# Loading the first batch alone, and projecting it in parts between the first attention items

## The chip, the cores and the metric

The kernel runs on one core of a Trainium2 chip. The metric is the device time of one execution in microseconds (us); before the change it is 2163.86 us, the median of three runs (2162.97 to 2166.31). The core has engines that run their own instruction queues side by side: TensorE for matrix products (PE in the profile, PEld for its weight loads), VectorE (DVE), ScalarE (ACT), GpSimd (POOL) and SyncE (SP), which here only issues transfers. ScalarE can issue transfers too. The queues meet through semaphores, on which an instruction waits for another engine or for a transfer to land.

## The reference, cut to what matters

The input `x` has 4 batches of 128 channels and 64 x 64 places, so N = 4096 tokens of 128 channels. Everything is in 32-bit floats.

```python
# layer 0: attention over all tokens, 64 inner channels
q, k, v = wq @ xf, wk @ xf, wv @ xf           # per batch: 64 x 4096
att = softmax(k.T @ q, axis=2)                # 4096 x 4096
x = x + wo @ (att @ v.T).T
# layer 1: tokens, layer norm, causal attention with 128 channels
t = tokens(x)
h = layer_norm(t)
t = t + softmax(causal((h @ Wq) @ (h @ Wk).T * 128**-0.5)) @ (h @ Wv)
# then a recurrence over the tokens
wx = batch_norm(layer_norm(t) @ W.T)          # statistics over all batches and tokens
y[i] = sigmoid(wx[i] + y[i-1] @ V.T)
out = from_tokens(t + y)
```

## The kernel before

The work is done in `fast_path`. A second path, `general_path`, runs only if a flag computed at the end says that the first one left its numeric range.

**Storage.** `xs` holds all four batches of `x` in on-chip memory, first as channels by tokens. Once the projections of a batch have read a block of 512 tokens, `tokens0` (L510) overwrites that block with the same data as tokens by channels, from a second input `xT`; the residual is added to it there. `kr` holds, for each half of the sequence, keys in one half of the partitions and rows (the queries' side) in the other; `swap` is a copy of `kr` with the two halves of the partitions exchanged, made by a transfer (L482), so that products over 64 channels can run on both halves of the array at once. `v` holds the values by tokens.

**Projections of a batch.** `keys(b, m)` (L750) returns three tasks for part `m` of four. Part `m` covers block `m` of 512 tokens and block `m + 4`. `cols0` multiplies both blocks by `wqk` and `wkq`, copies the results into `kr` by VectorE and ScalarE and starts the two `swap` transfers. `vals0` computes values, `vals0_by_tokens` transposes them. All of these take their PSUM tiles from `misc`, a ring of two buffers.

**Items.** The attention of both layers is cut into items: one block of 512 rows (`g`) against two tiles of 128 keys. Layer 0 of a batch has 8 blocks of 16 items; item `k` uses key tiles `k` and `k + 16`, so items 0 to 3 of a block need part 0 of the projections, items 4 to 7 part 1, and so on. Layer 1 follows for the same batch, and then the next batch. The loop at L774 goes over slots. In each, `scores` of item `s` (products and the exponential), `values` of item `s - 2`, and `sums` of item `s` are written out. At a block's last item, `rows()` (L764) prepares the block after the next, and for layer 0 also starts its token load; `finish0` or `finish1` are put into `waiting` to run a few slots later. A slot with nothing due takes one task from the list `side`. In the kernel before, the projections of batches 1 to 3 go through `side` during block 1 of the previous batch's layer 1 (L779 to L781), and those of batch 0 are all written ahead of the loop (L758 to L760).

**The opening.** Weights are loaded by ScalarE's queue (L398), `x` in sixteen loads of 512 KB by SyncE's queue (L407 to L409), all batches at once. The first product on TensorE is layer 1's combined weight `g1` = `wqT` times `wkT` (L453 to L455), read first by `rows1` in layer 1. The order of instructions on each engine is chosen by a scheduler that goes by the order of the program and by what is ready.

Of the kernel before, what the change touches and what calls it, by code (L numbers as in the profile page):

```python
# [9 lines left out]
F32 = mybir.dt.float32  # L10
# [5 lines left out]
P = 128  # L16
BLK = 512
CHUNK = 1024
# [331 lines left out]
def fast_path(  # L350
# [21 lines left out]
    nc = tc.nc  # L372
    B, C, N = x.shape
    M = c_wqT.shape[1]
    assert C == P and M == P // 2 and N % CHUNK == 0
    NT = N // P
    NB = N // BLK
# [7 lines left out]
    const = ctx.enter_context(tc.tile_pool(name="const", bufs=1))  # L385
# [5 lines left out]
    xs = xpool.tile([P, B, N], F32, name="xs")  # L391

    x2 = dram.tile([B, N, P], F32, name="x2")

    def load(name, shape, *parts):
        t = const.tile(shape, F32, name=name)
        for dst, src in parts:
            nc.scalar.dma_start(out=dst(t), in_=src)  # L398
        return t

    whole = lambda t: t
    lo, hi = (lambda t: t[:, 0:M]), (lambda t: t[:, M:P])
    top, bottom = (lambda t: t[0:M]), (lambda t: t[M:P])
    wqk = load("wqk", [P, P], (lo, c_wqT), (hi, c_wkT))
    wkq = load("wkq", [P, P], (lo, c_wkT), (hi, c_wqT))
    wv0 = load("wv0", [P, M], (whole, c_wvT))
    for b in range(B):  # L407
        for g in range(N // CHUNK):
            nc.sync.dma_start(out=xs[:, b, ts(g, CHUNK)], in_=x[b, :, ts(g, CHUNK)])  # L409
    wo2 = load("wo2", [P, P], (top, c_woT), (bottom, c_woT))  # L410
    wqT = load("wqT", [P, P], (whole, a_wqT))
    wkT = load("wkT", [P, P], (whole, a_wkT))
    wv1 = load("wv1", [P, P], (whole, a_wv))
    wf = load("wf", [P, P], (whole, f_wT))
    vf = load("vf", [P, P], (whole, f_vT))
    gamma = load("gamma", [P, 1], (whole, f_gamma))
    beta = load("beta", [P, 1], (whole, f_beta))

    ident = const.tile([P, P], F32, name="ident")
    make_identity(nc, ident)  # L420
# [5 lines left out]
    nc.gpsimd.memset(mhalf, -0.5)  # L426
    minus = const.tile([P, P], F32, name="minus")
    nc.vector.tensor_scalar(minus, ident, -1.0, None, ALU.mult)
    good = const.tile([P, 1], F32, name="good")
    g1 = const.tile([P, P], F32, name="g1")  # L430
    recs = const.tile([P, 2, B, NT], F32, name="recs")
# [10 lines left out]
    with tc.tile_pool(name="batch", bufs=1) as batch, tc.tile_pool(name="rows", bufs=2) as rowp, tc.tile_pool(  # L442
        name="prob", bufs=4
    ) as prob, tc.tile_pool(name="work", bufs=2) as wk, tc.tile_pool(name="stat", bufs=4) as stat, tc.tile_pool(
        name="ps_s", bufs=2, space=PSUM
    ) as ps_s, tc.tile_pool(name="ps_a", bufs=1, space=PSUM) as ps_a, tc.tile_pool(
        name="ps_m", bufs=2, space=PSUM
    ) as ps_m:

        def misc(name):  # L450
            return ps_m.tile([P, BLK], F32, tag="m", name=name)

        gp = misc("g_ps")  # L453
        nc.tensor.matmul(gp[:, :P], lhsT=wqT, rhs=wkT, start=True, stop=True)
        nc.vector.tensor_copy(g1, gp[:, :P])  # L455

        class Batch:
            pass
# [1 line left out]
        bs = [Batch() for _ in range(B)]  # L460
# [4 lines left out]
        def cols0(b, m):  # L465

            bt = bs[b]
            if m == 0:  # L470
                bt.kr = batch.tile([P, 2, N // 2], F32, tag="kr", name="kr")
                bt.swap = batch.tile([P, N // 2], F32, tag="swap", name="swap")
                bt.v = batch.tile([P, NT, M], F32, tag="v", name="v0")
            for h, w in enumerate((wqk, wkq)):
                ps = misc("kr_ps")
                nc.tensor.matmul(ps, lhsT=w, rhs=xs[:, b, ts(m + h * NB // 2, BLK)], start=True, stop=True)
                if h:
                    nc.scalar.copy(bt.kr[:, h, ts(m, BLK)], ps)
                else:
                    nc.vector.tensor_copy(bt.kr[:, h, ts(m, BLK)], ps)  # L480
                rows, keys = slice(M - h * M, P - h * M), slice(h * M, h * M + M)
                nc.sync.dma_start(out=bt.swap[keys, ts(m, BLK)], in_=bt.kr[rows, h, ts(m, BLK)])  # L482

        def vals0(b, m):

            ps = misc("v_ps")
            for h in range(2):
                nc.tensor.matmul(
                    ps[h * M : h * M + M], lhsT=wv0, rhs=xs[:, b, ts(m + h * NB // 2, BLK)], start=True, stop=True
                )  # L490
            vT = wk.tile([P, BLK], F32, tag="vT", name="vT")
            nc.scalar.copy(vT, ps)
            return vT

        def vals0_by_tokens(b, m, vT):
            ps = misc("vT_ps")
            for j in range(TPB):
                nc.tensor.transpose(ps[:, ts(j, P)], vT[:, ts(j, P)], ident)
            v = bs[b].v.rearrange("p (h t) c -> p t h c", h=2)[:, ts(m, TPB)]
            nc.scalar.copy(v, ps.rearrange("p (t h c) -> p t h c", h=2, c=M))  # L500
# [9 lines left out]
        def tokens0(b, g):  # L510

            nc.sync.dma_start(
                out=xs[:, b, ts(g, BLK)].rearrange("p (j c) -> p j c", c=P),
                in_=xT[b, ts(g, BLK)].rearrange("(j p) c -> p j c", p=P),
            )
# [111 lines left out]
        items, blocks = [], []  # L627
# [58 lines left out]
        def sums(it):  # L686

            if it.first:
                bs[it.b].dsum = wk.tile([P, 2, BLK], F32, tag="dsum", name="dsum")
            it.den = den = bs[it.b].dsum  # L690
            if all(n == BLK for _, _, n, _ in it.at):
                flat = den.rearrange("p a b -> p (a b)")
                if it.first:
                    nc.vector.tensor_copy(flat, it.p)  # L694
                else:
                    nc.vector.tensor_tensor(flat, flat, it.p, ALU.add)  # L696
                return
            for h, (t, q0, n, o) in enumerate(it.at):
                if it.first:
                    if q0:  # L700
                        nc.gpsimd.memset(den[:, h, :q0], 0.0)
                    nc.vector.tensor_copy(den[:, h, q0:], it.p[:, o : o + n])
                else:
                    nc.vector.tensor_tensor(den[:, h, q0:], den[:, h, q0:], it.p[:, o : o + n], ALU.add)  # L704
# [40 lines left out]
        def push(slot, chain):  # L745
            step = next(chain, None)
            if step:
                waiting.append((slot + step[0], step[1], chain))

        def keys(b, m):  # L750
            mem = []
            return [
                lambda: cols0(b, m),
                lambda: mem.append(vals0(b, m)),
                lambda: vals0_by_tokens(b, m, mem[0]),
            ]

        for m in range(NB // 2):  # L758
            for task in keys(0, m):
                task()  # L760
        SKEW = 2
        side = []

        def rows():  # L764

            if blocks:
                layer, b, g = blocks.pop(0)
                (rows1 if layer else rows0)(b, g)
                if layer == 0:
                    tokens0(b, g)  # L770

        rows()
        rows()
        for s in range(len(items) + SKEW + 16):  # L774
            if s < len(items):
                it = items[s]
                if it.first:
                    bs[it.b].rows = bs[it.b].next.pop(0)
                    if it.layer and it.g == 1 and it.b + 1 < B:  # L779
                        for m in range(NB // 2):  # L780
                            side += keys(it.b + 1, m)  # L781
                scores(it)
            if 0 <= s - SKEW < len(items):
                it = items[s - SKEW]
                values(it)
                if it.last:
                    rows()
                    if fill:
                        fill.pop(0)()
                    push(s, (finish1 if it.layer else finish0)(it.b, it.g))  # L790
            if s < len(items):
                sums(items[s])
            due = [w for w in waiting if w[0] <= s]
            if due:
                w = min(due, key=lambda w: w[0])
                waiting.remove(w)
                w[1]()
                push(s, w[2])
            elif side:
                side.pop(0)()  # L800
        assert not waiting and not side and not fill


# [4 lines left out]
    with tc.tile_pool(name="xr", bufs=1) as xrp, tc.tile_pool(name="y", bufs=2) as yp, tc.tile_pool(  # L808
        name="ps_y", bufs=1, space=PSUM
# [21 lines left out]
        start = xrp.tile([P, B, NCH + 1], F32, name="start")  # L831
# [130 lines left out]
```

## Time and profile before

| | |
|---|---|
| time, median of three | 2163.86 us |
| profiled span | 2161.9 us |
| `x` loads: number, size, median issue to landing | 16, 512 KB, 7.7 us |
| token loads `xT`: number, size, median | 32, 256 KB, 3.3 us |
| `swap` transfers: number, size, median | 32, 128 KB, 2.2 us |
| exponential of layer 0, 128x1024 (L670): mean | 1116 ns |
| running sums, 128x1024 (L696): mean | 1225 ns |
| score and value records of layer 0, 64x512 (L656, L716): mean | 593 and 591 ns |

A line of the timeline gives the start in us, the busy time in us, the engine, the line of the kernel, the operation, what it writes and reads, its shape, and how many instructions are merged in it; in brackets stands how long the engine was idle before it and who released it. "SPq" and "ACTq" are transfers being issued by SyncE and ScalarE. One 32-bit product appears as two PE records. Records overlap: a 512-column record lasts 592 ns, but the next begins 0.43 us after it. The table of stretches gives the stretch, its length, then for each engine the busy time and the count, then the granted clock, the busy share of the transfer engines and what they moved. The 128 KB of `swap` counts one transfer of L482.

### The profile page before, as it was taken

To read this page: it belongs to the slowest core of one execution; us is meant where nothing else is said; L and a number is where in the kernel's file an instruction comes from. 1 tells how busy PE (TensorE), PEld (TensorE's weight loads), DVE (VectorE), ACT (ScalarE), POOL (GpSimd) and SP (SyncE) were. 2 spreads that over 40 slices of the span, in tenths; PEclk is the share of its full clock that TensorE was granted. 3 is DMA by queue.
4 is the path that set the end of the run, shared out by engine and by line. 5 is a ranking of instruction groups with operands and counts; after the bars stand their busy time and mean duration, and the time that the engine had idled before them with its cause. 6 is when DMAs were issued, how large, how long until landed. Compare 5 with 4: busy or idle time off the path is not lost. (4 is left out here: it accounts for less than half of the span.)

```text
span 2161.9 us, 30424 instructions
## 1 busy us (share of the span) xinstructions
PE 2115.7 (98%) x12204; PEld 941.5 (44%) x12204; DVE 1435.2 (66%) x2703; ACT 1007.9 (47%) x1098; POOL 104.5 (5%) x207
## 2 busy tenths in 40 slices
PE   7999999999999999999999999999999999999978
PEld 2333354444333344444333335444433334544446
DVE  3888865444788876554588886544478887654468
ACT  4666633323566643333466663323356664333255
POOL 0000010000000010000000001000000001000000
PEclk9999999999999999999999999999999999999989
DMA  6000011000000001100000001100000000000033
GB/s 224 2 1 2 1 30 49 5 6 5 6 2 1 1 20 30 34 5 5 6 1 2 1 1 30 49 5 5 5 6 2 1 2 6 10 10 5 5 161 157
DMA packets 42997, 48.72 MB, mean 23 GB/s; under 512 B 3168, under 2 KB 36704, under 8 KB 40800
## 3 DMA queue, kind: packets, MB, share of 16 engines
q1 hardware_dynamic: 40960, 46.15, 6.4%
q8 instruction: 97, 1.59, 0.3%
q10 hardware_dynamic: 1888, 0.56, 0.1%
q14 instruction: 52, 0.43, 0.1%
HBM read 25.72 MB, written 16.78 MB: 20 GB/s over the span
## 5 line engine op out<-in xcount | busy, mean ns | idle before, releaser
L696 DVE TENSOR_TENSOR dsum<-dsum,p 128x1024 f32<-128x1024 f32 x676 | 827.9, 1225 | 464.3 <-ACT p L672 335.4
L670 ACT ACTIVATE p<-s_ps,nshift 128x1024 f32<-128x1024 f32 x512 | 571.2, 1116 | 357.7 <-PE s_ps L656 338.2
L672 ACT ACTIVATE p<-s_ps 128x1024 f32<-128x1024 f32 (+2 forms) x288 | 274.2, 952 | 598.8 <-PE s_ps L665 496.1
L716 PE MATMUL acc<-p,v 64*64 64x512 f32 x4096 | 533.2, 591 | 1.7 <-ACT half L735 1.7
L656 PE MATMUL s_ps<-swap,kr 64*64 64x512 f32 x2048 | 528.5, 593 | 0.4 <-ACT p L670 0.4
L656 PE MATMUL s_ps<-kr 64*64 64x512 f32 x2048 | 528.5, 593 | 0.0
L665 PE MATMUL s_ps<-rows,xhT 128*128 128x512 f32 (+3 forms) x1152 | 503.9, 559 | 0.0
L724 PE MATMUL acc<-p,xh 128*128 128x512 f32 (+3 forms) x1152 | 501.5, 557 | 0.0
L724 PEld LDWEIGHTS acc<-p,xh 128*128 128x128 f32 x1152 | 215.6, 190 | 241.3 <-issue 231.8
L665 PEld LDWEIGHTS s_ps<-rows,xhT 128*128 128x128 f32 x1152 | 211.0, 190 | 227.1 <-issue 189.7
L716 PEld LDWEIGHTS acc<-p,v 64*64 64x64 f32 x4096 | 155.2, 133 | 284.8 <-issue 265.8
L656 PEld LDWEIGHTS s_ps<-swap,kr 64*64 64x64 f32 x2048 | 137.0, 133 | 131.3 <-issue 124.2
L656 PEld LDWEIGHTS s_ps<-kr 64*64 64x64 f32 x2048 | 137.0, 133 | 128.3 <-issue 123.7
L436 POOL TENSOR_TENSOR ln_rstd<-ln_var,mhalf 128x4 f32<-128x4 f32 x64 | 66.1, 1033 | 1217.8 <-DVE ln_var L551 1217.8
L704 DVE TENSOR_TENSOR dsum<-dsum,p 128x256 f32<-128x256 f32 (+1 forms) x120 | 56.0, 499 | 72.0 <-POOL p L676 72.0
L694 DVE COPY dsum<-p 128x1024 f32<-128x1024 f32 x60 | 41.4, 690 | 66.8 <-ACT p L672 57.1
L539 DVE SCALAR_TENSOR_TENSOR xs<-o_ps,recs,xs 128x128 f32<-128x128 f32 x256 | 73.0, 345 | 8.9 <-PE o_ps L534 2.8
L555 DVE TENSOR_SCALAR xh<-xs,ln_mv,ln_rstd 128x128 f32<-128x128 f32 x256 | 71.4, 343 | 2.2
L676 POOL TENSOR_SCALAR_AFFINE_SELECT p<-p 128x128 f32<-128x128 f32 x128 | 34.4, 293 | 672.7 <-ACT p L672 672.7
L548 DVE BATCH_NORM_STATS2 ln_st<-xs 128x6 f32<-128x128 f32 x256 | 63.6, 271 | 0.0
L861 DVE SCALAR_TENSOR_TENSOR z<-xs,scale,y_ps 128x256 f32<-128x256 f32 x108 | 48.6, 481 | 6.7 <-PE y_ps L859 5.4
L614 ACT COPY xs<-wx_ps 128x512 f32<-128x512 f32 x32 | 18.7, 585 | 73.1 <-DVE stats L612 73.1
(104 smaller groups left out, 1058.7 us busy)
## 6 DMA issues: line engine op xcount, KB each, us to landing
xs<-in_x SPq DMA_DIRECT2D x16, 512.0 KB, 7.7
xs<-in_xT SPq DMA_DIRECT2D x32, 256.0 KB, 3.3
x<-xs SPq DMA_DIRECT2D x32, 256.0 KB, 2.3
xr<-x SPq DMA_DIRECT2D x8, 1024.0 KB, 11.9
out_x<-xr SPq DMA_DIRECT2D x8, 1024.0 KB, 4.4
swap<-kr SPq DMA_DIRECT2D x32, 128.0 KB, 2.2
wo<-in_c_woT ACTq DMA_DIRECT2D x2, 32.0 KB, 4.3
wqT<-in_a_wqT ACTq DMA_DIRECT2D x1, 64.0 KB, 5.2
```

What stands on the lines that cost most here:

```text
L436: nc.gpsimd.tensor_tensor(y, var, mhalf[:, : y.shape[-1]], ALU.pow)
L539: nc.vector.scalar_tensor_tensor(t, in0=op[:, ts(j, P)], scalar=rec[:, j : j + 1], in1=t, op0=ALU.mult, op1=ALU.add)
L548: nc.vector.bn_stats(st[:, j], xs[:, b, ds(g * BLK + j * P, P)])
L555: nc.vector.tensor_scalar(dst[:, j], xs[:, b, ds(g * BLK + j * P, P)], mv[:, j, 0:1], y[:, j : j + 1], ALU.subtract, ALU.mult)
L656: nc.tensor.matmul(ps[c * M : c * M + M, off : off + n], lhsT=bs[it.b].kr[part, h, ds(t % (NT // 2) * P + c * M, M)], rhs=rows[h], start=True,
L665: nc.tensor.matmul(ps[:, off : off + n], lhsT=lhsT, rhs=rhs, start=True, stop=True)
L670: nc.scalar.activation(it.p[:, :off], ps[:, :off], AF.Exp, bias=nshift)
L672: nc.scalar.activation(it.p[:, :off], ps[:, :off], AF.Exp, scale=float(P) ** -0.5)
L696: nc.vector.tensor_tensor(flat, flat, it.p, ALU.add)
L704: nc.vector.tensor_tensor(den[:, h, q0:], den[:, h, q0:], it.p[:, o : o + n], ALU.add)
L716: nc.tensor.matmul(bt.acc[h * M : h * M + M, r], lhsT=bt.v[part, t], rhs=it.p[part, o : o + n], start=it.first, stop=it.last,)
L724: nc.tensor.matmul(bt.acc[:, 0, q0:], lhsT=bt.xh[:, t], rhs=it.p[:, o : o + n], start=it.first and h == 0, stop=it.last and h == 1,)
```

## The change

At the start only batch 0 is loaded, in eight loads of 512 tokens, ordered by the parts of the projection that need them. The loads of `wo2`, `wqT`, `wkT` and `wv1` move from ScalarE's to SyncE's queue, behind `x`; `wf`, `vf`, `gamma` and `beta` are loaded later, by `load_rest`. The next batch's `x` is loaded while layer 0 of the current batch is at work: a small GpSimd copy out of `agg` into the region that the load will overwrite makes the load wait until that block's result exists. Twelve products of the identity with itself, whose result nothing reads, occupy TensorE until `x` comes. Of batch 0's projections only part 0 and the keys of part 1 are written ahead of the loop; the rest goes into `side`, one task a slot in the first block, and last `form`, which computes `g1`. The token loads of the first two blocks of batch 0 are put off until these tasks are done. The purpose is to let the items start sooner.

```diff
-    def load(name, shape, *parts):
+    def load(engine, name, shape, *parts):
...
-    for b in range(B):
-        for g in range(N // CHUNK):
-            nc.sync.dma_start(out=xs[:, b, ts(g, CHUNK)], in_=x[b, :, ts(g, CHUNK)])
...
+    for m in range(NB // 2):
+        for g in (m, m + NB // 2):
+            nc.sync.dma_start(out=xs[:, 0, ts(g, BLK)], in_=x[0, :, ts(g, BLK)])
+    wo2 = load(nc.sync, "wo2", [P, P], (top, c_woT), (bottom, c_woT))
+    wqT = load(nc.sync, "wqT", [P, P], (whole, a_wqT))
+    wkT = load(nc.sync, "wkT", [P, P], (whole, a_wkT))
+    wv1 = load(nc.sync, "wv1", [P, P], (whole, a_wv))
...
-        gp = misc("g_ps")
-        nc.tensor.matmul(gp[:, :P], lhsT=wqT, rhs=wkT, start=True, stop=True)
-        nc.vector.tensor_copy(g1, gp[:, :P])
+        wp = misc("warm_ps")
+        for _ in range(12):
+            nc.tensor.matmul(wp[:, :P], lhsT=ident, rhs=ident, start=True, stop=True)
+
+        def form():
+            gp = misc("g_ps")
+            nc.tensor.matmul(gp[:, :P], lhsT=wqT, rhs=wkT, start=True, stop=True)
+            nc.vector.tensor_copy(g1, gp[:, :P])
+
+        def load_rest():
+            for t, src in ((wf, f_wT), (vf, f_vT), (gamma, f_gamma), (beta, f_beta)):
+                nc.sync.dma_start(out=t, in_=src)
...
-        for m in range(NB // 2):
-            for task in keys(0, m):
-                task()
+        parts = [keys(0, m) for m in range(NB // 2)]
+        for task in parts[0][:2] + parts[1][:1] + parts[0][2:]:
+            task()
         SKEW = 2
-        side = []
+        side = parts[1][1:] + parts[2] + parts[3] + [form]
...
                 if layer == 0:
-                    tokens0(b, g)
-
+                    started.append((b, g))
+
+        def tokens():
+
+            while started:
+                b, g = started.pop(0)
+                tokens0(b, g)
+                if g == 2 and b + 1 < B:
+
+                    nc.gpsimd.tensor_copy(
+                        xs[:, b + 1].rearrange("p (k n) -> p k n", n=CHUNK)[:, :, 0], bs[b].agg[:, : N // CHUNK]
+                    )
+                    for k in range(N // CHUNK):
+                        nc.sync.dma_start(out=xs[:, b + 1, ts(k, CHUNK)], in_=x[b + 1, :, ts(k, CHUNK)])
...
                 if it.last:
                     rows()
+                    tokens()
...
             elif side:
                 side.pop(0)()
+                if not side and items[s].b == 0 and items[s].layer == 0:
+                    tokens()
+                    load_rest()
```

More of the change, by code (lines that the diff above doesn't have):

```diff
@@ L393, in fast_path @@
     x2 = dram.tile([B, N, P], F32, name="x2")
-    def load(name, shape, *parts):
+    def load(engine, name, shape, *parts):
         t = const.tile(shape, F32, name=name)
         for dst, src in parts:
-            nc.scalar.dma_start(out=dst(t), in_=src)
+            engine.dma_start(out=dst(t), in_=src)
         return t
@@ L403, in fast_path @@
     top, bottom = (lambda t: t[0:M]), (lambda t: t[M:P])
-    wqk = load("wqk", [P, P], (lo, c_wqT), (hi, c_wkT))
-    wkq = load("wkq", [P, P], (lo, c_wkT), (hi, c_wqT))
-    wv0 = load("wv0", [P, M], (whole, c_wvT))
-    for b in range(B):
-        for g in range(N // CHUNK):
-            nc.sync.dma_start(out=xs[:, b, ts(g, CHUNK)], in_=x[b, :, ts(g, CHUNK)])
[L410 to L417, printed above, removed]
+    wqk = load(nc.scalar, "wqk", [P, P], (lo, c_wqT), (hi, c_wkT))
+    wkq = load(nc.scalar, "wkq", [P, P], (lo, c_wkT), (hi, c_wqT))
+    wv0 = load(nc.scalar, "wv0", [P, M], (whole, c_wvT))
+    for m in range(NB // 2):
[5 more added lines that the diff above has]
+    wv1 = load(nc.sync, "wv1", [P, P], (whole, a_wv))
     ident = const.tile([P, P], F32, name="ident")
@@ L428, in fast_path @@
     nc.vector.tensor_scalar(minus, ident, -1.0, None, ALU.mult)
+    wf = const.tile([P, P], F32, name="wf")
+    vf = const.tile([P, P], F32, name="vf")
+    gamma = const.tile([P, 1], F32, name="gamma")
+    beta = const.tile([P, 1], F32, name="beta")
     good = const.tile([P, 1], F32, name="good")
@@ L769, in rows @@
                 if layer == 0:
-                    tokens0(b, g)
+                    started.append((b, g))
[9 more added lines that the diff above has]
+                        nc.sync.dma_start(out=xs[:, b + 1, ts(k, CHUNK)], in_=x[b + 1, :, ts(k, CHUNK)])
+        started = []
         rows()
```

## The prediction

> **What bounds the kernel now.** I read the page first: the busy shares and the forty slices of the span.
>
> ```profile
> PE 2115.7 (98%) x12204; PEld 941.5 (44%) x12204; DVE 1435.2 (66%) x2703; ACT 1007.9 (47%) x1098; POOL 104.5 (5%) x207
> ...
> PE   7999999999999999999999999999999999999978
> ...
> DMA  6000011000000001100000001100000000000033
> ```
>
> TensorE is busy 98% of the span, so only the slices where its digit is below 9 can give time back: the first one, and the last two, which the change does not touch. The first slice (54 us) is also the only early one in which the DMA engines are busy. Next I asked for the busy time of each engine in three stretches of the first 60 us; columns are PE, weight loads, VectorE, ScalarE, GpSimd, clock, DMA share, GB/s.
>
> ```profile
> 0.00:12.20 12.20, 0.00 (x0) 0.00 (x0) 0.00 (x0) 0.00 (x0) 0.81 (x9) 1.00 0.77 237
> 12.20:32.40 20.20, 17.08 (x50) 5.87 (x50) 3.19 (x6) 7.72 (x12) 0.00 (x0) 1.00 0.95 336
> 32.40:60.00 27.60, 27.16 (x253) 9.60 (x256) 18.42 (x16) 18.31 (x18) 0.00 (x0) 1.00 0.32 88
> ```
>
> TensorE does nothing for 12.2 us, then 20.2 us of projections, and from 32.4 us runs nearly gapless. The timeline and the waits of the opening say why:
>
> ```profile
> 12.27 0.77 PE L454 MATMUL g_ps<-wkT,wqT 128*128 128x128 f32 x2 [12.27 <-DMA wkT<-in_a_wkT]
> 12.83 1.92 PE L476 MATMUL kr_ps<-xs,wqk 128*128 128x512 f32 x2
> ...
> 19.16 0.63 PE L498 MATMUL vT_ps<-ident,vT 128*128 128x128 f32 x4 [0.80 <-ACT vT L492]
> 19.62 1.02 PE L476 MATMUL kr_ps<-xs,wqk 128*128 128x512 f32 x2
> ...
> 32.42 0.14 PEld L656 LDWEIGHTS s_ps<-swap,kr 64*64 64x64 f32 x2 [0.22 <-DMA swap<-kr]
> ...
> 34.80 0.65 PE L656 MATMUL s_ps<-swap,kr 64*64 64x512 f32 x2 [0.44 <-ACT p L670]
> ```
>
> Three things hold the start. (a) The first matmul is layer 1's combined weight `g1`, which waits for `wkT`, landed only at 12.2. (b) Four projection parts then run one after another, each stretched by its PSUM evacuations: parts start at 19.62, 23.80 and 28.04, 4.2 us each, for 3.0 us of matmuls. The first part takes 6.8 us because TensorE is cold. (c) The first score needs the first `swap` transfer. It was issued at 21.66, behind all sixteen loads of `x` on SyncE's queue, and took 10.7 us: landed 32.36, almost the moment it was used. Part (c) means that speeding the projections alone would give nothing; all of `x` had to move first.
>
> **What the Trainium skill says.** "TensorE: Matmul & The Clock Gate", section "Part 1: The HAM clock gate", says that an idle array runs at half clock until about 3.4 us of sustained work. The trace agrees on the ratio (a 512-column record is 1062 ns at 12.83 and 592 ns at 19.62), less on the time: all of 12.27 to 18.4 is still slow, over 6 us. The measurement decides; I keep 3.4 as a lower end. "DMA: Bandwidth & Descriptors", section "Anatomy of one DMA", puts a fixed cost of about 2.0 us on a transfer (given there for another issue path). The page's median for the 128 KB `swap` is 2.2 us, so the 10.7 us of the first is queueing.
>
> **The change part by part.**
>
> *Loads.* Only batch 0 (2 MB) and 0.42 MB of weights are asked for at the start. Issue times in the trace show transfers waiting for earlier ones: loads of `x` at 0.80 and 1.2, the third at 5.0 when the first had landed, the fourth at 6.5 when the second had, then 9.4 and 12.2. Counting both queues, the transfer that had to land is the eighth before, so I read it as eight in flight. After the change there are 18 transfers ahead of the swap. The first eight land by about 4 to 7 us, the rest are issued 4 to 8 us; 2.4 MB at the 237 GB/s of the first stretch would be 10 us, at 336 GB/s 7 us, plus 2 us of start. The two blocks of part 0 come first.
>
> *Warm-up.* Twelve 128-column products make 24 records. Their input `ident` is ready at 1.43 us (last GpSimd piece 1.14 + 0.29), so I start them at 1.6. Cold spacing is 0.28 us (the two `g_ps` records run from 12.27 to 12.83), warm 0.124 (eight 128-column `o_ps` records from 67.01 to 68.00, 0.99 us). All cold: 24 x 0.28 = 6.7, end 8.3. Warm after 3.4 us: 12 x 0.28 + 12 x 0.124 = 4.9, end 6.5. The weights `wqk` landed at 1.25 + 5.5 = 6.75. So the first real product starts between 6.75 and 8.3; **I take 7.5**, at full clock. What waits behind the warm-ups is only that product.
>
> *Opening.* Order is now keys of part 0, values of part 0, keys of part 1, transposes of part 0. Using part 2's warm spacing and two PSUM buffers: keys at +0 and +0.86; copies end +1.75 (DVE) and +2.58 (ACT); values +1.90, copied by +3.63; keys of part 1 at +2.76 and +3.69; transposes once DVE has freed a buffer, +4.66 to +5.10. So the scores can begin at 7.5 + 5.1 = 12.6. The swap they need: copied at 9.25, issued 9.4, landing 2.2 to 3.0 later (3.0 is the last swap in the trace), 11.6 to 12.4. Just hidden.
>
> *Moved work.* Nine tasks leave the opening and run one per item in the first block: three values (0.86), three sets of transposes (0.43), two sets of keys (1.71), `form` (two records, 0.25). Sum 2.58 + 1.29 + 3.42 + 0.25 = 7.5 us, now between full TensorE work and so at full price. Do they stall? In the trace the same tasks of batch 1 run inside layer 1 gapless (keys at 312.50, next scores at 314.22, exactly 2 x 0.86). A slot there and here is 1.72 us of matmuls; ACT has 1.11 us of exp and DVE 1.23 us of sums in it, so a copy of 0.58 or 0.69 fits. I allow 0.9 us of stalls. Against it, before had 0.6 us idle ahead of the third item (33.76 + 0.43 to 34.80) which a task now fills. Net cost 0.3.
>
> *Held-back batches, token loads, `load_rest`, the 128x4 GpSimd copy.* Nothing on the path: batch 1's `x` starts after the first block, about 50 us, and is read first at 312; the copy is one of GpSimd's small operations (at most the 1033 ns of `ln_rstd`, at least a 100 ns memset), beside a GpSimd 5% busy; a block's tokens are first read by its finish, four items into the next block (in before at 69.08 for block 0), long after their issue; the later weights are read in layer 1.
>
> *Sum.* Scores start 32.4 - 12.6 = 19.8 us earlier; 7.5 are paid back in the first block and 0.3 in stalls: gain 12.0. From 2163.9: **2152** us. With the first product at 6.75, the gain is 12.8; at 8.3 and with a cold microsecond left, about 10.2.
>
> **The rivals.**
>
> *The swap becomes the start again.* SyncE's queue holds thirteen loads ahead of it. If the eight-in-flight limit keeps them until 12.2, as it kept the sixth load of `x` in before, the swap lands near 15, and the gain is 32.4 - 15 - 7.8 = 9.6: 2154.3. For it: the stalls of the issues above. Against: a quarter of the `x` bytes.
>
> *The moved tasks stall TensorE.* In the old opening each part idled 1.2 us beyond its 3.0 us. If the three parts' worth of tasks keep that, 3.6 us are lost: 2155.6. Against it: the gapless layer 1 tasks.
>
> *Loads land early.* With less traffic the weights land at 5.5, and the clock is up by then: gain 14, 2150.
>
> *Held-back loads block the tokens (slower).* They share SyncE's in-order queue with the token loads, wait there for a GpSimd copy, and bring 2 MB, 6 us at 336 GB/s. If in each of three batches a block's finish waits for tokens behind them, 18 us are lost: 2164 - 12 + 18 = 2170. Against it: a block of items lasts 27 us, and the tokens are wanted one or two blocks later.
>
> **How the numbers follow.** Forecast 0.68, swap 0.14, stalling tasks 0.06, early loads 0.08, blocked tokens 0.04. The range takes the first four with the ends of the forecast's own unknowns: 2149.5 to 2157. The 0.2% bound is 4.3 us, so the first four cases are all faster, except a small part of the second and third if both strike (0.02). Faster 0.95, same 0.02, slower 0.03.
>
> **What would show it.** Right: warm-ups from about 1.6 us, first `kr_ps` near 7.5 with records of about 592 ns, first `s_ps` near 12.6, and the first block 7.5 us longer than its 16 x 1.72; the rest of the trace shifted as a whole. Wrong step by step: 1062 ns records in the opening (clock), the first score released by the swap later than 13 (queue), idle TensorE around the moved tasks, or a wait on `in_xT` at the blocks' ends. Idle time that first appears after the first block would make the forecast wrong altogether.

## The result, and the profile after

The changed kernel takes 2155.93 us (median, 2154.90 to 2157.25), the kernel before 2164.49 us beside it: a ratio of 0.996 with a 95% interval of 0.9943 to 0.9978. Run again later it took 2156.96 us, ratio 0.9969 (0.9957 to 0.9981). The gain is some 7 to 8.6 us; 12 had been forecast.

First the busy shares and the slices of the page, as for the kernel before:

```profile
PE 2117.8 (98%) x12228; PEld 943.8 (44%) x12228; DVE 1434.3 (67%) x2703; ACT 1007.7 (47%) x1098; POOL 105.1 (5%) x210
...
PE   9999999999999999999999999999999999999978
...
DMA  3100011000100001000010001100000000000033
```

The first digit of TensorE rose from 7 to 9, which is as much as this view can say: it counts the warm-ups, whose result nothing reads, and counts slow products at their full length. The `x` loads are now three more humps in the DMA row. The timeline of TensorE says more:

```profile
1.49 4.86 PE L457 MATMUL warm_ps<-ident 128*128 128x128 f32 x24 [1.49 <-POOL ident masks.py:199]
6.19 1.02 PE L487 MATMUL kr_ps<-xs,wqk 128*128 128x512 f32 x2
7.05 1.02 PE L487 MATMUL kr_ps<-xs,wkq 128*128 128x512 f32 x2
8.00 1.08 PE L499 MATMUL v_ps<-xs,wv 128*64 128x512 f32 x4
9.01 1.12 PE L487 MATMUL kr_ps<-xs,wqk 128*128 128x512 f32 x2
9.98 1.02 PE L487 MATMUL kr_ps<-xs,wkq 128*128 128x512 f32 x2
10.92 0.66 PE L509 MATMUL vT_ps<-ident,vT 128*128 128x128 f32 x4
14.86 0.65 PE L667 MATMUL s_ps<-swap,kr 64*64 64x512 f32 x2 [3.28 <-DMA swap<-kr]
...
15.91 1.97 PE L499 MATMUL v_ps<-xs,wv 128*64 128x512 f32 x4
17.82 1.12 PE L667 MATMUL s_ps<-swap,kr 64*64 64x512 f32 x2
```

The first product of the projections runs at 6.19 instead of 12.83, at full clock, and the opening is over at 11.58. Then TensorE stands still for 3.28 us, for the first `swap` transfer, and after that its records are slow: the values of part 1 take 1.97 us where 1.08 is usual, the scores 1.12 instead of 0.65. The granted clock of the profile is 0.50 from 15.78 to 19.20, and 1.00 from 11.58 to 15.78 and from 19.20 to 25. (At the very start the clock column does not tell: it is 1.00 in before from 12.20 to 32.40, though the records up to 18.4 are slow.) VectorE's copy and SyncE's queue tell why the transfer is late:

```profile
7.25 0.69 DVE L491 COPY kr<-kr_ps 128x512 f32<-128x512 f32 x1 [5.55 <-PE kr_ps L487]
...
9.22 0.43 SPq L398 DMA_DIRECT2D wv<-in_a_wv  x1
10.02 0.33 SPq L466 DMA_DIRECT2D wf<-in_f_wT  x1
10.91 0.33 SPq L466 DMA_DIRECT2D vf<-in_f_vT  x1
11.65 0.33 SPq L466 DMA_DIRECT2D gamma<-in_f_gamma  x1
12.02 0.43 SPq L466 DMA_DIRECT2D beta<-in_f_beta  x1
12.57 0.50 SPq L493 DMA_DIRECT2D swap<-kr  x1
```

`kr` was ready at 7.94 (7.25 + 0.69), but its transfer was issued at 12.57, behind thirteen loads that the text puts there and four that it doesn't. `load_rest` is written in the loop, after nine items; but its loads wait for nothing, and the scheduler took them forward, ahead of the swap. So "later" in the text did not make them later.

A mark for the opening is ScalarE's first copy into `half`, at the end of block 0. It comes at 62.72 before:

```profile
62.72 1.00 ACT L735 COPY half<-acc 128x1024 f32<-128x1024 f32 x1
```

and at 56.56 after:

```profile
56.56 1.00 ACT L746 COPY half<-acc 128x1024 f32<-128x1024 f32 x1
```

So the opening gained 6.16 us. From the first score to this mark before took 30.30 us (62.72 - 32.42), after 41.70 us (56.56 - 14.86), that is 11.40 more. The start came 17.56 us earlier (32.42 - 14.86), and 17.56 - 11.40 = 6.16. The rest of the time's gain arises later and is taken up below.

### The profile page after: what moved, and what is told of

The parts are those of the page before. It is cut to its first block, busy times and chain, and to the rows that moved or that the text cites. A ratio compares the mean times of both kernels' runs of the same rounds, so it can differ in the third digit from the quotient of the medians.

```text
span 2153.5 us, 30500 instructions
## 1 busy us (share of the span) xinstructions
PE 2117.8 (98%) x12228; PEld 943.8 (44%) x12228; DVE 1434.3 (67%) x2703; ACT 1007.7 (47%) x1098; POOL 105.1 (5%) x210
```

## The experiments

Each ran at least five times beside the kernel before. The table gives the first product of the projections, the issue of the first swap, the first score, the `half` mark (us from the start of the profile), and the median time.

| kernel | product | swap | score | mark | time |
|---|---|---|---|---|---|
| before | 12.83 | 21.66 | 32.42 | 62.72 | 2163.1 to 2164.5 |
| changed | 6.19 | 12.57 | 14.86 | 56.56 | 2155.93 |
| changed, again | 6.61 | 12.96 | 15.26 | 56.96 | 2156.96 |
| four loads after the swap | 6.78 | 9.74 | 12.75 | 52.87 | 2152.64 |
| nine loads after the swap | 6.18 | 7.96 | 12.01 | 52.12 | 2152.32 |
| the wait filled | 6.38 | 12.71 | 15.00 | 55.11 | 2155.02 |
| nine after, no warm-up | 5.89 | 8.69 | 13.76 | 53.88 | 2154.50 |
| changed, no warm-up | 5.77 | 10.61 | 14.38 | 53.33 | 2153.44 |
| all projections in front | 6.30 | 12.65 | 23.14 | 53.44 | 2152.67 |
| in front, in turn | 6.08 | 12.38 | 21.34 | 51.64 | 2151.45 |
| all of `x` at once | 6.77 | 25.79 | 30.56 | 61.98 | 2162.68 |

**The order of the queue.** Two kernels issue the same transfers in another order; `issue_after` only fixes the place in SyncE's queue and adds no wait.

```diff
-                nc.sync.dma_start(out=bt.swap[keys, ts(m, BLK)], in_=bt.kr[rows, h, ts(m, BLK)])
+                swaps.append(nc.sync.dma_start(out=bt.swap[keys, ts(m, BLK)], in_=bt.kr[rows, h, ts(m, BLK)]))
...
         def load_rest():
+            with tc.issue_after(swaps[0].ins):
                 for t, src in ((wf, f_wT), (vf, f_vT), (gamma, f_gamma), (beta, f_beta)):
                     nc.sync.dma_start(out=t, in_=src)
```

> Edit: the same transfers as in the changed kernel, but wf, vf, gamma and beta are issued on SyncE's queue after the first swap transfer instead of ahead of it. Theory A (the swap waits in SyncE's queue, and the 3.3 us wait lets TensorE's clock drop): the first swap is issued near 9.7 us instead of 12.57, lands near 11.9, the first score starts there instead of at 14.86, and the 1.1 us records after it are gone; the first block's half copy comes at 56.6 - 3.0 - 1.9 = 51.7; time 2151, some 5 us less than the changed kernel. Rival B (the swap is late because the transfer engines are busy with the loads, whatever the order): landing near 14 as before, time 2155 to 2156. Rival C (the tasks moved into the first block eat the gain, the start is not what limits): the start moves by 3 us but the half copy by under 1 us; time 2155.

The swap was issued at 9.74, as soon as the queue was free, and the time fell to 2152.64 us, ratio 0.995 (0.9937 to 0.9964); all its runs (2152.13 to 2153.38) lie below all of the changed kernel's. In the timeline, the wait is short and the records after it are at full clock:

```profile
11.64 0.66 PE L512 MATMUL vT_ps<-ident,vT 128*128 128x128 f32 x4
12.75 0.65 PE L670 MATMUL s_ps<-swap,kr 64*64 64x512 f32 x2 [0.45 <-DMA swap<-kr]
...
13.77 1.08 PE L502 MATMUL v_ps<-xs,wv 128*64 128x512 f32 x4
```

The mark moved by 3.69 us and not 4.9. The swap now took 3.0 us instead of 2.2, so the score came 2.1 us earlier and not 3.0, and the slow records had cost 1.6 us and not 1.9, as the filled wait below shows. B and C fall. In the second kernel `wo2`, `wqT`, `wkT` and `wv1` follow the swap too, and their loads at the start are deleted:

```diff
         for task in parts[0][:2] + parts[1][:1] + parts[0][2:]:
             task()
+        with tc.issue_after(swaps[0].ins):
+            for dst, src in ((wo2[0:M], c_woT), (wo2[M:P], c_woT), (wqT, a_wqT), (wkT, a_wkT), (wv1, a_wv)):
+                nc.sync.dma_start(out=dst, in_=src)
```

> Edit: as the run before, and also wo2, wqT, wkT and wv1 behind the first swap, so that only the eight loads of x stand ahead of it. Theory A: swap issued near 8.0, landed by 10.5, so the first score follows the transposes at about 11.5 with no wait; half copy near 51.2; time 2150.5. Rival B: as the changed kernel, 2155 to 2156. Rival C: start moves by 3.4 us, half copy by under 1 us.

2152.32 us, 0.9954 (0.9941 to 0.9968). The swap was issued at 7.96 as expected, but took 4.0 us, with blocks of `x` still under way, and landed at 12.0. So TensorE still waits for it:

```profile
10.91 0.66 PE L509 MATMUL vT_ps<-ident,vT 128*128 128x128 f32 x4
12.01 0.65 PE L667 MATMUL s_ps<-swap,kr 64*64 64x512 f32 x2 [0.44 <-DMA swap<-kr]
```

In both kernels the score starts when the swap lands, and the 0.75 us between their marks is the 0.74 us between their first scores. That B explains a part of the wait, once the queue is short, was not expected. The times of the two (2152.13 to 2153.38 and 2152.00 to 2154.86) do not separate.

**The wait and the clock apart.** Twelve more unread products between the transposes and the first score (whose products were also fixed behind them in TensorE's queue):

```diff
+        wp2 = misc("fill_ps")
+        for _ in range(12):
+            filler = nc.tensor.matmul(
+                wp2[:, :P], lhsT=bs[0].kr[:, 1, BLK : BLK + P], rhs=ident, start=True, stop=True
+            )
```

> Edit: the changed kernel with twelve more products that nothing reads, between the transposes of part 0 and the first score, to keep TensorE busy while it waits for the swap. It takes the clock's part from the wait's part. Theory A: first score still at 14.86, but its records stay near 0.6 us instead of 1.1; half copy 1.9 us earlier, 54.7; time 2154. Rival (the slow records come from the change of product shape from 128 to 64 rows and columns, or from ScalarE's late exponentials): no change, half copy 56.6, time 2156.

2155.02 us, 0.9961 (0.9947 to 0.9974). The score still waits for the swap, at 15.00, and the slow records are gone:

```profile
11.86 2.94 PE L774 MATMUL fill_ps<-ident,kr 128*128 128x128 f32 x24
15.00 0.65 PE L667 MATMUL s_ps<-swap,kr 64*64 64x512 f32 x2 [0.19 <-DMA swap<-kr]
...
16.02 1.08 PE L499 MATMUL v_ps<-xs,wv 128*64 128x512 f32 x4
```

From first score to mark it takes 40.11 us, against 41.70: the clock cost the changed kernel 1.6 us, close to half of the 3.42 us that it stood at 0.50. Both kernels with the other queue order take 40.11 or 40.12 as well.

**The warm-ups.** The kernel with nine loads behind the swap, without the warm-up products (the three lines of `warm_ps` deleted):

> Edit: the second run of this call without the twelve warm-up products. Theory A (the warm-ups pay because nothing else then hides a cold start): first product near 5.4 us but with 1062 ns records until about 11.5; transposes end near 13, first score there instead of at 11.5; time 1.5 to 2.3 us above the second run, 2152 to 2153. Rival (the warm-ups only delay the first product, which waits for them at 6.1): the same time as the second run or 0.5 us less.

2154.50 us, 2.2 us above the same kernel with them; the mark is 1.76 us later. The first product came at 5.89, with slow records:

```profile
5.89 2.04 PE L484 MATMUL kr_ps<-xs,wqk 128*128 128x512 f32 x2 [5.89 <-DMA wqk<-in_c_wkT]
7.73 1.58 PE L484 MATMUL kr_ps<-xs,wkq 128*128 128x512 f32 x2
9.24 1.08 PE L496 MATMUL v_ps<-xs,wv 128*64 128x512 f32 x4
```

The clock was up by 9.24, earlier than expected, but the swap then took 5.0 us. The transposes start at 12.25 instead of 10.91, so 1.3 of the 1.76 us are the slow products, and the rest comes with the later swap. The totals alone say less: two of the five runs with warm-ups took 2154.72 and 2154.86. The warm-ups pay by the mark. The same deletion in the changed kernel:

> Edit: the changed kernel without the twelve warm-up products, nothing else in the text; the scheduler then happens to put the swap transfers ahead of wf, vf, gamma and beta. Theory A (the queue order costs the changed kernel more than the warm-ups gain): first product near 5.9 with slow records, swap issued near 9.7, first score near 13.8, half copy near 54, time 2154 to 2155, below the changed kernel. Rival (the warm-ups are worth their 2 us whatever the order): half copy 58, time 2158.

2153.44 us, 3.5 us less than the changed kernel beside it. The products are slow again, yet without the warm-ups the scheduler put the swaps first: issued at 10.61 instead of 12.57. Here a useful part of the change looked harmful, because taking it out moved something else. Only the pair above measures the warm-ups.

**Splitting the projections.** All four parts ahead of the first score, with the loads of the changed kernel:

```diff
-        for task in parts[0][:2] + parts[1][:1] + parts[0][2:]:
+        for task in [t for part in parts for t in part]:
             task()
...
-        side = parts[1][1:] + parts[2] + parts[3] + [form]
+        side = [form]
```

(The first item's scores were also fixed behind the last transposes in TensorE's queue.)

> Edit: the changed kernel, but all four parts of batch 0's projections stand ahead of the first score again, as in before; loads and their order as in the changed kernel; only the product for g1 stays in the first block. Theory A (the gain is the earlier loads; moving the tasks into the block pays back their full price and more): first product near 6.2, parts 4.2 us apart, first score near 22.7 with no wait and no slow records; the block then takes 30.3 us as in before plus 0.5, so the half copy comes near 53.5, 3 us before the changed kernel's 56.56; time 2153. Rival (the split is what gains, since it hides the copies between the projection products): half copy at 60 or later, time 2159 or more.

2152.67 us, 0.9949 (0.9935 to 0.9963), with the mark at 53.44, both as A said. The swap lands while projections run, and from the first score to the mark it takes 30.30 us, as before. So in the changed kernel as it stands the split brings nothing: it lost 3 us in the opening. That is the split with its late swap and slow records. With the swap ahead of nine loads its mark was 52.12, 1.3 us earlier than here, though the times (2152.32 and 2152.67) do not separate. What TensorE lost with all parts in front is in its waits between 5 and 24 us:

```profile
PE vT_ps L511 <- ACT vT L505: 3.0, 4, 0.8
```

Four waits for ScalarE's copies. The last kernel puts other products there:

```diff
-        for task in [t for part in parts for t in part]:
+        k, v, t = zip(*parts)
+        for task in (k[0], v[0], k[1], t[0], v[1], k[2], t[1], v[2], k[3], t[2], v[3], t[3]):
             task()
```

> Edit: as the run with all projections in front, but the next part's keys stand ahead of a part's transposes, so that TensorE has a product to do while ScalarE copies. Theory A (an idle TensorE between the parts, 1.2 us a part, is the cost of the old opening, and switching between products of 128 and of 64 rows is the cost of the split one; this form has neither): the opening takes about 14 us instead of 16.8, first score near 20.3, block 30.3, half copy near 50.6, time 2150, the least of all. Rival (ScalarE's three copies a part set the pace in any order): first score near 23, half copy 53.4, time 2152.7 as with all in front.

2151.45 us (2150.94 to 2152.10), 0.9946 (0.9933 to 0.996): the least of all, and below both given kernels. Three of the four waits are gone, the opening takes 15.3 us (6.08 to 21.34) instead of 16.8, and the mark is at 51.64. A saw the direction and overrated it by 1 us, of which 0.77 is the last part, which has no following keys to hide its copy behind:

```profile
18.90 1.08 PE L501 MATMUL v_ps<-xs,wv 128*64 128x512 f32 x4
20.75 0.66 PE L511 MATMUL vT_ps<-ident,vT 128*128 128x128 f32 x4 [0.77 <-ACT vT L505]
21.34 0.65 PE L669 MATMUL s_ps<-swap,kr 64*64 64x512 f32 x2
```

**The held-back loads.** The changed kernel with batches 1 to 3 loaded behind batch 0:

```diff
+    for b in range(1, B):
+        for k in range(N // CHUNK):
+            nc.sync.dma_start(out=xs[:, b, ts(k, CHUNK)], in_=x[b, :, ts(k, CHUNK)])
     wo2 = load(nc.sync, "wo2", [P, P], (top, c_woT), (bottom, c_woT))
...
-                if g == 2 and b + 1 < B:
-                    nc.gpsimd.tensor_copy(
...
```

> Edit: the changed kernel, but batches 1 to 3 are loaded at the start, behind batch 0 and ahead of the other weights; nothing is held back. TensorE's order then has all projections ahead of the first score. Theory A (holding the loads back is what frees the swap): first product still near 6.2, but the swap lands near 31 and the first score waits for it some 8 us; half copy near 63, time near 2164, as before the change. Rival (the gain is the early first product and the warm clock, and the held-back loads only matter for bandwidth): first score near 23, half copy near 54, time 2154.

2162.68 us, 0.9994 (0.9986 to 1.0002): nothing is left of the gain, though the first product comes at 6.77. The opening's products end near 23.2, and then

```profile
22.58 0.66 PE L512 MATMUL vT_ps<-ident,vT 128*128 128x128 f32 x4 [0.77 <-ACT vT L506]
29.87 0.76 PE L464 MATMUL g_ps<-wkT,wqT 128*128 128x128 f32 x2 [6.64 <-DMA wkT<-in_a_wkT]
30.56 1.12 PE L670 MATMUL s_ps<-swap,kr 64*64 64x512 f32 x2
```

The wait ends with `wkT`, since the scheduler set `form` ahead of the scores here; the first swap, issued at 25.79 and 4.3 us under way, landed at 30.1, only just later. Either is held by the twelve loads ahead of it.

**How much is steady.** The changed kernel once more:

> The changed kernel once more, as it is, to see how much of its 8.6 us is steady. The opening alone brought the first half copy from 62.72 to 56.56, which is 6.2 us; 2.2 us of the two profiles' difference arise later, in a slow spell of the clock near 1570 us and in the recurrence. If these are chance, the half copy repeats at 56.5 to 57 and the gain in time lies nearer 7 than 8.6, 2156 to 2157; if they belong to the change, the gain repeats at 8.6 and the later stretches repeat too.

The mark repeats (56.96; again 41.70 us after the first score), the time is 2156.96 and the gain 6.8 us. The two profiles of the first comparison differ by 8.4 us, of which 6.16 lie in the opening. Another 0.7 us is a slow spell in batch 3's first block. In before

```profile
1576.39 1.10 PE L563 MATMUL xh2T_ps<-ident,xh 128*128 128x128 f32 x4 [1.48 <-DVE xh L555]
...
1578.51 1.95 PE L716 MATMUL acc<-p,v 64*64 64x512 f32 x8
```

and in the changed kernel, at the same place in the program,

```profile
1570.22 1.10 PE L574 MATMUL xh2T_ps<-ident,xh 128*128 128x128 f32 x4 [1.47 <-DVE xh L566]
...
1572.16 1.04 PE L727 MATMUL acc<-p,v 64*64 64x512 f32 x8
```

The granted clock there is 0.50 for 3.41 us in before and 1.00 throughout in the changed kernel. All eleven profiles have the same wait of 1.47 or 1.48 us at each of the three changes of batch, near 545, 1057 and 1570. Eight have one such spell of 3.41 us after one of the three: the first in four of the runs (four loads after the swap, nine, the wait filled, in front in turn), the second in nine after without warm-up, and the third in before, all in front and all of `x` at once. The changed kernel, its repeat and the changed kernel without warm-up have none there. From the mark to the last copy of `agg` it takes 2000.15 or 2000.16 us in these three and 2000.88 to 2000.92 in the eight.

The other 1.5 us lie after the last attention block: from the last copy of `agg` to the end it is 98.3 us in before, 96.8 in the changed kernel, 97.1 in its repeat, and 97.1 to 98.1 in the other eight, whose program is the same there. Every profile has a spell of 17.07 us at clock 0.50 in that stretch. It begins 6.05 us after the copy in before and 3.64 us after it in the changed kernel, and in the eleven profiles a later begin goes, by and large, with a longer stretch. I read both as chance of the clock: the spells move between kernels whose program is the same at those places. No run repeats one kernel often enough to show it.

## Why the prediction was right or wrong

The measured time lies in the range and on the forecast side, but the forecast's own case did not happen: the gain was 7 to 8.6 us, not 12. The range held because it took in the rivals. The swap was late, and the moved tasks cost more than their products; both together had stood in the forecast only beside a chance of 0.02. The slow clock after the wait, for which I had no term, came on top.

**What bounded the kernel: right.** The three holds of the start, and above all (c), the swap behind all loads of `x`. Loading everything at once again took the whole gain away.

**Warm-up: right in kind, the first product 1.3 us too late in the forecast.** I took 7.5; it was 6.19. The weights landed earlier with less traffic (5.35: issued at 1.25, 4.1 us), and the 24 records took 4.86 us, near the lower end of 4.9, which came from the 3.4 us of the Trainium skill ("TensorE: Matmul & The Clock Gate", "Part 1: The HAM clock gate"). In other runs they took 4.76 to 5.49 us.

**Opening: right.** 5.1 us were forecast and it took 5.4.

**The swap: the step that failed.** "Just hidden" supposed it issued right after its copy. It waited 4.6 us for its turn. I had counted the thirteen loads on SyncE's queue, made a rival of them at 0.14 with the score at 15 and the time at 2154.3, and this rival's number is what happened: 14.86. That it fits so well is partly luck, for its cause was only partly mine. With thirteen loads ahead the swap went at 9.74 (the first order experiment) and the score came at 12.75 after a wait of 0.45 us; it was the four loads of `load_rest`, costed at nothing under "not on the path", that made the wait of 3.28. I took their place in the text for their place in the queue. Of the 2.8 us that they held the swap, 1.3 us are waits of their issues for loads of `x` to land, which fits the limit that the rival named. The forecast also had no price for what a wait does to the clock afterwards, 1.6 us.

**Moved work: the kind right, the cost beyond the products mis-sized.** I keep the 7.5 us of products as counted; for stalls I allowed 0.9 and took 0.6 back. Free of the clock, the block took 40.11 us against 30.30, so 9.8 us, and the net term is 2.3 instead of 0.3. The model for it, batch 1's tasks in layer 1, was the wrong one. There, keys between scores run at 0.86 us a product. In layer 0's block, in the kernel with nine loads behind the swap:

```profile
25.69 1.04 PE L727 MATMUL acc<-p,v 64*64 64x512 f32 x8
26.66 1.13 PE L487 MATMUL kr_ps<-xs,wqk 128*128 128x512 f32 x2
27.62 1.02 PE L487 MATMUL kr_ps<-xs,wkq 128*128 128x512 f32 x2
28.57 0.65 PE L667 MATMUL s_ps<-swap,kr 64*64 64x512 f32 x2
```

the starts are 0.97, 0.96 and 0.95 us apart, each 0.1 above 0.86, with no wait in between. Layer 0's scores and values are products on 64x64 pieces of the array, keys use all of it. "TensorEngine Tiling (Array Packing)", section "Key Properties", says that changing the tiling mode drains TensorE; the trace fits it with 0.1 us at the passages into and out of a task. The step from `wqk` to `wkq`, where the mode stays, seems to belong to the passage ahead of it: the opening of the changed kernel, shown above, has it too. There `wqk` takes 1.02 us and `wkq` starts 0.86 later where the warm-ups, 128*128 like it, went ahead (6.19), but 1.12 and 0.97 where `v_ps`, 128*64, went ahead (9.01). So it is the first product after a change of shape that is longer by 0.1 us. No run takes the tiling alone away, so this part stays a reading. That all of the 9.8 us goes when the tasks stay in front is shown (30.30 us twice).

**The sum.** Forecast: 19.8 - 7.5 - 0.3 = 12.0. Measured in the opening: 17.56 - 7.5 - 2.3 - 1.6 = 6.2. What I read as chance of the clock, 2.2 us between the two profiles of the first comparison, was in none of my terms.

**The other rivals.** Tasks that cost more than their products were there with 2.3 of the 3.6 us, though not as idle time: TensorE was busy around them. Early loads happened in part and were lost again in the wait. No wait for tokens appears; the loads of batch 1 start at 58.80, after the first block, as argued.

## What to carry to other kernels

A load that waits for nothing can be issued early wherever the text puts it. If a short transfer on the critical path shares a queue with loads, look up the queue's actual order, or tie the loads to what they must follow. Work moved out of an opening into a full engine was paid at full price there and at a little more; putting the opening's own products into its gaps was slightly cheaper (mark 51.64 against 52.12 us for the best split, time 2151.45 against 2152.32). And compare two versions by a mark close to the edit before reading microseconds in the total: here the total carried some 2 us that arose elsewhere.

## What the runs showed of the hardware that was not expected

A wait of 3.28 us was followed by half the granted clock within a microsecond of its end, for 3.42 us; in the repeat the same came 1.4 us after the end of a wait of 3.26. A wait of 1.47 or 1.48 us, of which each profile has three, was followed by 3.41 us at half clock in 8 of the 33 cases. The waits of 0.44 and 0.45 us for the swap were followed by none. In the wait of 6.64 us with all of `x` loaded at once, the clock went down 4.1 us after the wait's begin.

The same 128 KB transfer took 2.2 us as it was issued at 12.57, with little else under way. It took 3.0, 4.0 and 5.0 us as it was issued at 9.74, 7.96 and 8.69 in other kernels, with larger loads still moving: issuing it 1.8 us earlier brought it 0.8 us (landed at 11.96 instead of 12.74).
